# Graph attention on one core: own-block weighing and norms on ScalarE, the addition of own blocks on VectorE

## The chip, the cores and the metric

The kernel runs on one core of a Trainium2 chip. Its engines work beside each other, each with its own queue that is worked through in order: TensorE (PE, with its weight loads PEld), VectorE (DVE), ScalarE (ACT), GpSimd (POOL), and SyncE (SP), which here only issues transfers. The metric is the device time of one launch in microseconds. The kernel before took 2456.25 us, the median of three runs.

## The reference

One layer of attention over a graph, added to its input and normalised. `x` is 16 x 1024 x 512 in float32, `adj` is a 1024 x 1024 matrix of zeros and ones, the same for all 16 batches; there are 8 heads of 64.

```python
q = (x @ Wq + bq).reshape(b, n, H, HD)
k = (x @ Wk + bk).reshape(b, n, H, HD)
v = (x @ Wv + bv).reshape(b, n, H, HD)
scores = jnp.einsum('bqhd,bkhd->bhqk', q, k) / jnp.sqrt(jnp.float32(HD))
scores = scores + (1.0 - adj)[None, None, :, :] * -1000000000.0
attn = jax.nn.softmax(scores, axis=-1)
out = jnp.einsum('bhqk,bkhd->bqhd', attn, v).reshape(b, n, d)
x = _layernorm(x + out @ Wo + bo, axis=-1)
```

The matrix is sparse: most rows have few ones, the first rows have the most.

## The kernel before

The kernel does not compute the full score matrix. It lists the edges (query, key) of `adj` once, at the start (`edges`), and then handles 128 edges at a time, in a *block*. The 1024 queries of a batch are eight tiles `t` of 128. A tile has two kinds of blocks. In an *own* block each of the tile's 128 queries stands on its own partition with one of its keys; there are `OWN = (7, 3, 3, 1, 1, 2, 2, 2)` of them per tile. The edges that are left over are packed densely into *sum* blocks, `BLOCKS = (5, 2, 1, 2, 2, 1, 1, 1)` per tile, in which a partition is some edge. That is 36 blocks a batch (21 own, 15 sum) and 576 in all, tiles of 12, 5, 4, 3, 3, 3, 3 and 3 blocks.

A batch's *front* makes q, k and v of each tile: PE transposes x (L388), multiplies by the three weights (L406, four matmuls for each product), DVE adds the biases to q and k (L428, L435), ACT copies v (L441), and SP writes the rows to `q_rows` and `kv_rows` in DRAM. `norm` (L413) computes the sums of squares of each row of q and k by head: ACT squares 512 columns (L417), and one step later DVE sums them by head (L418). Their maximum is used only at the end, in a guard that chooses a general path if the scores could be too large; the values are never large here.

A block then goes through these steps. `gather` (L539, L544) issues from POOL the indirect transfers of k and v rows (`kvg`), and of q rows (`qg`) for a sum block; an own block uses the tile's q rows as they are (`qt`). `scores` multiplies q by k (L559) and sums by head (L561) on DVE. `exponentials` (L571) makes exp on ACT into the last 8 columns of the block's tile `pv`; the first block of a query tile takes `pv` from a ring of two buffers (`pv0`), all others from a ring of `PV_BUFS`. `weigh` multiplies v by these eight weights: one DVE instruction (L582), or eight on ACT, one for each head (L578). Before the change ACT does this in the first batch for odd blocks and in the last batch for two of three. An own block is added to the tile's first own block by `add_own`, on POOL (L594); a sum block goes to `add_up`, two pairs of matmuls into PSUM (L603, L604), with a 0/1 matrix that sends each edge to its query.

`normalise` adds the two parts and divides (L610 to L617, DVE), PE transposes the result (L622), ACT copies it (L626), and `finish` multiplies by Wo (L406, `po`), adds `y`, which is x + bo (POOL, L492; DVE, L499), and normalises the rows (DVE L502 to L505, POOL L508 to L510, ACT L513).

The order of the work on every engine is written by hand, by a loop over steps `n`. Step `n` emits: gathers up to block `n + 8`; `weigh(n + 1)`; `scores(n + 2)`; `normalise` of the previous tile, if block `n` is the first of a tile; whatever earlier steps have planned for this one (`later(k, fn)`); `exponentials(n + 2)`; and `add_up(n)` or `add_own(n)`. Then PE gets as much work of fronts and finishes as a credit in microseconds allows, `share` per step, with constants for the cost of each unit (`PRODUCT`, `SUM`, `TRANSPOSE`). The fronts run more than a batch ahead of the blocks and end with the mean row of v (L463 on ACT), once per batch; 34 lead-in steps come before block 0.

Of the kernel before, what the change touches and what calls it, by code (L numbers as in the profile page):

```python
# [23 lines left out]
OWN = (7, 3, 3, 1, 1, 2, 2, 2)  # L24
# [1 line left out]
DEGREE = (80, 16, 16, 16, 16, 16, 16, 16)  # L26

AHEAD = 8
KG_BUFS, QG_BUFS, QT_BUFS, PV_BUFS = 8, 5, 3, 4
NO_ROW = 65536.0  # L30

ROWS = 3
# [9 lines left out]
P = 128  # L42
# [99 lines left out]
def kernel(  # L142
# [33 lines left out]
    nc = tc.nc  # L176
    B, N, D = x.shape
    HD = D // HEADS
# [26 lines left out]
    with ExitStack() as main:  # L205
# [75 lines left out]
        def later(k, fn):  # L281
            plan.setdefault(now[0] + k, []).append(fn)
# [130 lines left out]
        def norm(b, t, i, s):  # L413
            if t == 0 and i == 0:
                NRM[b] = work.tile([P, 2, NT, HEADS], F32, tag="nrm", name=f"nrm_{b}", bufs=2)
            sq = work.tile([P, D], F32, tag="sq", name=f"sq_{b}_{t}_{i}", bufs=2)
            nc.scalar.activation(sq, s, AF.Square)  # L417
            later(1, lambda: nc.vector.tensor_reduce(  # L418
                NRM[b][:, i, t, :], sq.rearrange("p (h d) -> p h d", d=HD), axis=AX.X, op=OP.add
            ))  # L420

        def front(b, t):

# [33 lines left out]
            def mean_pe():  # L457
                p = fill_psum(f"pm_{b}")
                nc.tensor.matmul(p[0:1, :], mean, VSUM.pop(b), start=True, stop=True)

                def out():
                    m = work.tile([1, D], F32, tag="sq", name=f"mean_{b}", bufs=2)
                    nc.scalar.copy(m, p[0:1, :])  # L463
# [88 lines left out]
        def scores(n):  # L552
            b, t, i = blocks[n]
            if i < OWN[t]:
                q = QT[b, t] if i < OWN[t] - 1 else QT.pop((b, t))
            else:
                q = QG.pop(n)
            m = work.tile([P, D], F32, tag="qk", name=f"qk_{n}", bufs=2)
            nc.vector.tensor_tensor(m, q, KG[n][:, 0:D], op=OP.mult)  # L559
            S[n] = small.tile([P, HEADS], F32, tag="s", name=f"s_{n}", bufs=3)  # L560
            nc.vector.tensor_reduce(S[n], m.rearrange("p (h d) -> p h d", d=HD), axis=AX.X, op=OP.add)  # L561

        def exponentials(n):

            b, t, i = blocks[n]
            if i == 0:
                PV[n] = work.tile([P, D + HEADS], F32, tag="pv0", name=f"pv_{n}", bufs=2)
            else:
                PV[n] = work.tile([P, D + HEADS], F32, tag="pv", name=f"pv_{n}", bufs=PV_BUFS)
            bias = absent[:, own[t] + i:own[t] + i + 1] if i < OWN[t] else 0.0  # L570
            nc.scalar.activation(PV[n][:, D:], S.pop(n), AF.Exp, bias=bias)  # L571

        def weigh(n):
            v, pv = KG.pop(n), PV[n]
            b, t, i = blocks[n]
            if (b == 0 and n % 2) or (b == B - 1 and n % 3):
                for h in range(HEADS):
                    nc.scalar.activation(  # L578
                        pv[:, ts(h, HD)], v[:, ds(D + h * HD, HD)], AF.Copy, scale=pv[:, D + h:D + h + 1]
                    )  # L580
                return
            nc.vector.tensor_tensor(  # L582
                pv[:, 0:D].rearrange("p (h d) -> p h d", d=HD),
                v[:, D:].rearrange("p (h d) -> p h d", d=HD),
                pv[:, D:, None].to_broadcast([P, HEADS, HD]), op=OP.mult,
            )

        def add_own(n):
            b, t, i = blocks[n]
            pv = PV.pop(n)  # L590
            if i == 0:
                PV[b, t] = pv
            else:
                nc.gpsimd.tensor_tensor(PV[b, t], PV[b, t], pv, op=OP.add)  # L594

        def add_up(n):
            b, t, i = blocks[n]
# [47 lines left out]
        with tc.manual_schedule():  # L645
# [12 lines left out]
            while n < total or plan or urgent or done or finishing:  # L658
# [8 lines left out]
                while gathered[0] < min(n + AHEAD + 1, total) and blocks[gathered[0]][0] in set_up:  # L667
                    gather(gathered[0])
                    gathered[0] += 1
                if 0 <= n + 1 < total:  # L670
                    weigh(n + 1)
                if 0 <= n + 2 < total:
                    scores(n + 2)
                if 1 <= n <= total and (n == total or blocks[n][2] == 0):
                    normalise(*blocks[n - 1][:2])
                for fn in plan.pop(n, ()):
                    fn()
                if 0 <= n + 2 < total:
                    exponentials(n + 2)
                credit += share  # L680
                if 0 <= n < total and blocks[n][2] >= OWN[blocks[n][1]]:
                    add_up(n)
                    credit -= SUM
                elif 0 <= n < total:
                    add_own(n)
                for tile_done in done[:1]:
                    if tile_done not in Y:
                        load_y(*tile_done)
# [75 lines left out]
```

## Time and profile before

| | us |
|---|---|
| runs | 2456.4, 2456.25, 2439.39 (median 2456.25) |
| profiled execution, its own time | 2437.71 |
| span of its instructions | 2435.9 |
| POOL busy | 1560.1 |
| ACT busy | 712.8 |
| mean granted clock of TensorE | 0.957 of full speed |

A profile row of a group gives line, engine, operation, what is written and read, the count, and then busy time in us, the mean of one in ns, the idle time before them and what ended it. A timeline row gives start and duration in us. A row of stretches gives the window, its length, busy time and count of PE, PEld, DVE, ACT and POOL in that order, then granted clock, share of the DMA engines and GB/s. A row of waits gives total, count and longest in us.

### The profile page before, as it was taken

Reading aid. Unit: us, or ns where it says so; the run is one execution under the profiler, and the core shown is the slowest. Engines: PE = TensorE matmul, PEld = TensorE weight load, DVE = VectorE, ACT = ScalarE, POOL = GpSimd, SP = SyncE. Lnnn points to the kernel's source line nnn. Section 1 sums busy time; section 2 is a strip of 40 time slices with the busy share of each in tenths; the row PEclk is TensorE's granted clock in tenths of the full one; section 3 lists DMA queues with packets and bytes.
Section 4 is the critical chain, followed back from the end, with each engine's and each line's share of the span. In section 5 each row is a group of like instructions: output and inputs, shape, how many; then the busy total and the mean of one; then the engine's idle time right before and its main releaser. Section 6 shows DMA issues by size and latency. Waiting matters only on the chain.

```text
span 2435.9 us, 23939 instructions
## 1 busy us (share of the span) xinstructions
PE 2204.7 (91%) x6185; PEld 1098.5 (45%) x6185; DVE 2198.2 (90%) x3606; ACT 712.8 (29%) x1746; POOL 1560.1 (64%) x1565
## 2 busy tenths in 40 slices
PE   6988999899999989999998999999999999988555
PEld 3434445454444545444454544445454444444232
DVE  6588999899999999999999999999999999999875
ACT  2345522222222222222222222222222222222253
POOL 1055676767667676666767666576766757676683
PEclk9989999999999999999999999999999999999768
DMA  4367678687777768777776877777786767767572
GB/s 164 112 212 237 227 266 265 219 292 240 258 238 263 251 212 297 231 259 230 269 253 216 288 235 261 233 263 250 231 294 220 275 224 271 250 214 268 174 257 69
DMA packets 216639, 577.65 MB, mean 237 GB/s; under 512 B 33695, under 2 KB 33707, under 8 KB 216494
## 3 DMA queue, kind: packets, MB, share of 16 engines
q0 software_dynamic: 102144, 331.89, 42.7%
q1 hardware_dynamic: 111776, 239.16, 27.4%
q10 hardware_dynamic: 2574, 4.99, 0.6%
q8 instruction: 51, 0.84, 0.1%
q14 instruction: 94, 0.77, 0.1%
HBM read 474.75 MB, written 134.26 MB: 250 GB/s over the span
## 4 chain that ended last, share of the span: by engine, by line
DVE 42%; PE 28%; issue 16%; POOL 7%; DMA 4%; ACT 2%; POOLq 0%; ACTq 0%; SPq 0%; DVEq 0%
DVE pv L582 9%; DVE qk L559 9%; PE pv L406 7%; PE pq L406 6%; PE pk L406 6%; DVE s L561 5%; PE po L406 3%; DVE stats L502 3%; POOL kvg L544 3%; DVE y L499 3%; DVE nrm L418 3%; POOL y L492 2%; DVE o L611 2%; PE sum L603 2%; PE sum L604 2%
## 5 line engine op out<-in xcount | busy, mean ns | idle before, releaser
L544 POOL DMA_INDIRECT kvg<-kv_rows,key_row x576 | 643.3, 1117 | 348.2 <-DVE pv L582 207.7
L582 DVE TENSOR_TENSOR pv<-kvg,pv 128x512 f32<-128x512 f32 x534 | 480.7, 900 | 40.1 <-ACT pv L571 36.8
L406 PE MATMUL po<-wo,oT 128*128 128x512 f32 x1024 | 504.1, 625 | 0.0
L406 PE MATMUL pq<-wq,xT 128*128 128x512 f32 x1024 | 481.4, 602 | 23.9 <-ACT xT L392 13.1
L406 PE MATMUL pv<-wv,xT 128*128 128x512 f32 x1024 | 487.2, 611 | 0.0
L406 PE MATMUL pk<-wk,xT 128*128 128x512 f32 x1024 | 472.3, 593 | 0.0
L561 DVE TENSOR_REDUCE s<-qk 128x8 f32<-128x512 f32 x576 | 395.2, 686 | 19.9
L539 POOL DMA_INDIRECT qg<-q_rows,query_row x240 | 277.9, 1158 | 49.3 <-issue 43.7
L406 PEld LDWEIGHTS pv<-wv,xT 128*128 128x128 f32 x1024 | 201.2, 198 | 220.5 <-issue 212.7
L406 PEld LDWEIGHTS po<-wo,oT 128*128 128x128 f32 x1024 | 199.2, 202 | 202.9 <-issue 196.7
L571 ACT ACTIVATE pv<-s,absent 128x8 f32<-128x8 f32 x336 | 101.1, 301 | 629.7 <-DVE s L561 514.5
L406 PEld LDWEIGHTS pk<-wk,xT 128*128 128x128 f32 x1024 | 191.2, 190 | 206.0 <-issue 201.4
L406 PEld LDWEIGHTS pq<-wq,xT 128*128 128x128 f32 x1024 | 188.3, 193 | 198.5 <-issue 170.3
L559 DVE TENSOR_TENSOR qk<-qt,kvg 128x512 f32<-128x512 f32 x336 | 271.8, 809 | 0.0
L594 POOL TENSOR_TENSOR pv<-pv,pv 128x520 f32<-128x520 f32 x208 | 269.6, 1296 | 3.2
L508 POOL TENSOR_TENSOR rstd<-rstd,neg_half 128x1 f32<-128x1 f32 x128 | 108.5, 848 | 208.0 <-DVE rstd L505 199.1
L492 POOL TENSOR_TENSOR y<-y,bo_bc 128x512 f32<-128x512 f32 x128 | 169.4, 1323 | 110.1 <-DMA y<-in_x_dram 108.0
L603 PE MATMUL sum<-pv,sums 128*128 128x256 f32 x480 | 154.4, 405 | 91.1 <-DVE pv L582 58.5
L571 ACT ACTIVATE pv<-s 128x8 f32<-128x8 f32 x240 | 50.0, 209 | 569.1 <-DVE s L561 465.7
L603 PEld LDWEIGHTS sum<-pv,sums 128*128 128x128 f32 x480 | 92.2, 199 | 210.2 <-issue 99.3
L418 DVE TENSOR_REDUCE nrm<-sq 128x8 f32<-128x512 f32 x256 | 172.8, 676 | 1.2 <-ACT sq L417 1.2
L617 DVE TENSOR_TENSOR o<-o,rden 128x512 f32<-128x512 f32 x128 | 167.3, 1307 | 4.4
(109 smaller groups left out, 2184.2 us busy)
## 6 DMA issues: line engine op xcount, KB each, us to landing
kv_rows<-kv SPq DMA_DIRECT2D x128, 512.0 KB
x<-in_x_dram SPq DMA_DIRECT2D x128, 256.0 KB
q_rows<-q SPq DMA_DIRECT2D x128, 256.0 KB
qt<-q_rows SPq DMA_DIRECT2D x128, 256.0 KB
y<-in_x_dram SPq DMA_DIRECT2D x128, 256.0 KB
out_dram<-y SPq DMA_DIRECT2D x128, 256.0 KB
kvg<-kv_rows,key_row POOLq DMA_INDIRECT x576
a<-in_adj_dram SPq DMA_DIRECT2D x8, 512.0 KB
```

The costliest lines, as they stand in the source:

```text
L406: nc.tensor.matmul(p, lhs()[:, ts(c, P)], w[:, c, :], start=(c == 0), stop=(c == NPAIR - 1))
L418: later(1, lambda: nc.vector.tensor_reduce(NRM[b][:, i, t, :], sq.rearrange("p (h d) -> p h d", d=HD), axis=AX.X, op=OP.add))
L492: later(2, lambda: nc.gpsimd.tensor_tensor(Y[b, t], Y[b, t], bo_bc, op=OP.add))
L539: nc.gpsimd.indirect_dma_start(out=QG[n], out_offset=None, in_=q_rows[b % ROWS], in_offset=bass.IndirectOffsetOnAxis(ap=query_row[:, g:g + ...
L544: nc.gpsimd.indirect_dma_start(out=KG[n], out_offset=None, in_=kv_rows[b % ROWS], in_offset=bass.IndirectOffsetOnAxis(ap=key_row[:, g:g + ...
L559: nc.vector.tensor_tensor(m, q, KG[n][:, 0:D], op=OP.mult)
L561: nc.vector.tensor_reduce(S[n], m.rearrange("p (h d) -> p h d", d=HD), axis=AX.X, op=OP.add)
L571: nc.scalar.activation(PV[n][:, D:], S.pop(n), AF.Exp, bias=bias)
L582: nc.vector.tensor_tensor(pv[:, 0:D].rearrange("p (h d) -> p h d", d=HD), v[:, D:].rearrange("p (h d) -> p h d", d=HD), pv[:, D:, None].to ...
L594: nc.gpsimd.tensor_tensor(PV[b, t], PV[b, t], pv, op=OP.add)
L603: nc.tensor.matmul(PSUM[b, t][:, 0, 0:HD2], m, pv[:, 0:HD2], **kw)
L617: nc.vector.tensor_tensor(o8, o8, r[:, :, None].to_broadcast([P, HEADS, HD]), op=OP.mult)
```

## The change

Five things change.

- `norm` squares each head's 64 columns by itself on ACT, with the sum of squares as the instruction's second output; DVE's reduction goes.
- `by_act` says which blocks ACT weighs: own blocks except each tile's first, in all batches, and in the last batch every fourth block as well. All others are weighed on DVE.
- `add_own` adds on DVE, not on POOL.
- The order within a step: `exponentials(n + 3)` comes first, DVE's weighing of `n + 1` is followed by `scores(n + 4)`, then the addition of own block `n`, and ACT's weighing of `n + 1` comes after the planned work.
- Rings: 9 buffers for gathered k and v, not 8; 6 for `pv`, not 4; 4 for scores, not 3. `pv0` keeps its two.

```diff
-KG_BUFS, QG_BUFS, QT_BUFS, PV_BUFS = 8, 5, 3, 4
+KG_BUFS, QG_BUFS, QT_BUFS, PV_BUFS = 9, 5, 3, 6
...
         def norm(b, t, i, s):
...
-            sq = work.tile([P, D], F32, tag="sq", name=f"sq_{b}_{t}_{i}", bufs=2)
-            nc.scalar.activation(sq, s, AF.Square)
-            later(1, lambda: nc.vector.tensor_reduce(
-                NRM[b][:, i, t, :], sq.rearrange("p (h d) -> p h d", d=HD), axis=AX.X, op=OP.add
-            ))
+            for h in range(HEADS):
+                sq = work.tile([P, HD], F32, tag="sq", name=f"sq_{b}_{t}_{i}_{h}", bufs=2)
+                nc.scalar.activation(sq, s[:, ts(h, HD)], AF.Square, accum_out=NRM[b][:, i, t, h:h + 1])
...
+        def by_act(n):
+            b, t, i = blocks[n]
+            return 0 < i < OWN[t] or (b == B - 1 and n % 4 == 0)
+
         def weigh(n):
             v, pv = KG.pop(n), PV[n]
-            b, t, i = blocks[n]
-            if (b == 0 and n % 2) or (b == B - 1 and n % 3):
+            if by_act(n):
                 for h in range(HEADS):
                     nc.scalar.activation(
                         pv[:, ts(h, HD)], v[:, ds(D + h * HD, HD)], AF.Copy, scale=pv[:, D + h:D + h + 1]
...
-                nc.gpsimd.tensor_tensor(PV[b, t], PV[b, t], pv, op=OP.add)
+                nc.vector.tensor_tensor(PV[b, t], PV[b, t], pv, op=OP.add)
...
-                if 0 <= n + 1 < total:
+                if 0 <= n + 3 < total:
+                    exponentials(n + 3)
+                if 0 <= n + 1 < total and not by_act(n + 1):
                     weigh(n + 1)
-                if 0 <= n + 2 < total:
-                    scores(n + 2)
+                if 0 <= n + 4 < total:
+                    scores(n + 4)
+                if 0 <= n < total and blocks[n][2] < OWN[blocks[n][1]]:
+                    add_own(n)
                 if 1 <= n <= total and (n == total or blocks[n][2] == 0):
                     normalise(*blocks[n - 1][:2])
                 for fn in plan.pop(n, ()):
                     fn()
-                if 0 <= n + 2 < total:
-                    exponentials(n + 2)
+                if 0 <= n + 1 < total and by_act(n + 1):
+                    weigh(n + 1)
...
-                elif 0 <= n < total:
-                    add_own(n)
```

Line numbers shift a little: in the changed kernel the product of q and k is L557, its reduction L559, the exponential L569, the weighing L579 (ACT) and L583 (DVE), the own addition L595, and the head's square L418.

Where instructions stand now is seen best in the seven own blocks of a batch's first tile; in the names `pv_146` the number is that of the block (144 is the first of batch 4), and the number behind it counts instructions. DVE before, in the steps of blocks 145 and 146:

```order
L582 TENSOR_TENSOR pv_146_5416<-kvg_146_5206,pv_146_5416 128x512
L559 TENSOR_TENSOR qk_147_5437<-qt_4_0_5143,kvg_147_5242 128x512
L561 TENSOR_REDUCE s_147_5439<-qk_147_5437 128x8
L452 TENSOR_TENSOR vsum_5_5283<-vsum_5_5283,kv_5_2_5344 128x512
L428 SCALAR_TENSOR_TENSOR q_5_3_5446<-pq_5_3_5425,bq_bc_102 128x512
L582 TENSOR_TENSOR pv_147_5449<-kvg_147_5242,pv_147_5449 128x512
L559 TENSOR_TENSOR qk_148_5469<-qt_4_0_5143,kvg_148_5271 128x512
L561 TENSOR_REDUCE s_148_5471<-qk_148_5469 128x8
```

DVE in the same two steps after the change:

```order
L557 TENSOR_TENSOR qk_149_6813<-qt_4_0_6445,kvg_149_6638 128x512
L559 TENSOR_REDUCE s_149_6815<-qk_149_6813 128x8
L595 TENSOR_TENSOR pv_144_6642<-pv_144_6642,pv_145_6679 128x520
L450 TENSOR_TENSOR vsum_5_6620<-vsum_5_6620,kv_5_2_6703 128x512
L426 SCALAR_TENSOR_TENSOR q_5_3_6823<-pq_5_3_6800,bq_bc_102 128x512
L557 TENSOR_TENSOR qk_150_6852<-qt_4_0_6445,kvg_150_6675 128x512
L559 TENSOR_REDUCE s_150_6854<-qk_150_6852 128x8
L595 TENSOR_TENSOR pv_144_6642<-pv_144_6642,pv_146_6721 128x520
```

The weighing (L582) is gone from these steps, the addition (L595) has come in behind the scores, and the scores are those of two blocks later.

ACT before, from the exponential of block 147 on:

```order
L571 ACTIVATE pv_147_5449<-s_147_5439,absent_111 128x8
L513 ACTIVATE y_3_5_5326<-y_3_5_5326,rstd_5383 128x512
L417 ACTIVATE sq_5_3_0_5476<-q_5_3_5446 128x512
L626 COPY oT_3_7_5478<-poT_3_7_5454 128x512
L571 ACTIVATE pv_148_5487<-s_148_5471,absent_111 128x8
L571 ACTIVATE pv_149_5512<-s_149_5504,absent_111 128x8
```

ACT after, in the same place (the squares of q's tile 3 of the next batch):

```order
L418 ACTIVATE sq_5_3_0_0_6860,nrm_5_6275<-q_5_3_6823 128x64
L418 ACTIVATE sq_5_3_0_1_6862,nrm_5_6275<-q_5_3_6823 128x64
L418 ACTIVATE sq_5_3_0_2_6864,nrm_5_6275<-q_5_3_6823 128x64
L418 ACTIVATE sq_5_3_0_3_6866,nrm_5_6275<-q_5_3_6823 128x64
L418 ACTIVATE sq_5_3_0_4_6868,nrm_5_6275<-q_5_3_6823 128x64
L418 ACTIVATE sq_5_3_0_5_6870,nrm_5_6275<-q_5_3_6823 128x64
L418 ACTIVATE sq_5_3_0_6_6872,nrm_5_6275<-q_5_3_6823 128x64
L418 ACTIVATE sq_5_3_0_7_6874,nrm_5_6275<-q_5_3_6823 128x64
L627 COPY oT_3_7_6876<-poT_3_7_6836 128x512
L579 ACTIVATE pv_147_6768<-kvg_147_6578,pv_147_6768 128x64 x8
L569 ACTIVATE pv_150_6904<-s_150_6854,absent_111 128x8
L579 ACTIVATE pv_148_6811<-kvg_148_6606,pv_148_6811 128x64 x8
```

One square has become eight, and eight weighing instructions stand at the end of a step, in front of the next step's exponential.

The second place is the start of a three-block tile. Block 168 is the first of tile 4, block 171 the first of tile 5, and `o_4_3` is the normalised tile 3, whose `pv_165` lies in the ring of two that `pv_171` takes. ACT before:

```order
L513 ACTIVATE y_4_1_5990<-y_4_1_5990,rstd_6046 128x512
L417 ACTIVATE sq_6_0_1_6138<-kv_6_0_6109 128x512
L441 COPY kv_6_0_6109<-pv_6_0_6089 128x512
L392 COPY xT_6_2_6142<-pxT_6_2_6117 128x512
L571 ACTIVATE pv_171_6146<-s_171_6134,absent_111 128x8
```

ACT after:

```order
L627 COPY oT_4_2_7665<-poT_4_2_7639 128x512
L569 ACTIVATE pv_171_7679<-s_171_7655,absent_111 128x8
L569 ACTIVATE pv_172_7712<-s_172_7684,absent_111 128x8
L511 ACTIVATE y_4_1_7559<-y_4_1_7559,rstd_7630 128x512
L418 ACTIVATE sq_6_0_1_0_7721,nrm_6_7608<-kv_6_0_7692 128x64
```

DVE after, in the step of block 168, whose normalisation reads `pv_165`:

```order
L583 TENSOR_TENSOR pv_169_7600<-kvg_169_7404,pv_169_7600 128x512
L557 TENSOR_TENSOR qk_172_7682<-qt_4_5_7476,kvg_172_7523 128x512
L559 TENSOR_REDUCE s_172_7684<-qk_172_7682 128x8
L611 TENSOR_TENSOR rden_4_3_7687<-sum_4_3_7632,pv_165_7441 128x8
L612 TENSOR_TENSOR o_4_3_7686<-sum_4_3_7632,pv_165_7441 128x512
```

The exponential of block 171 has moved from the end of step 169 to the head of step 168, and its buffer is that of `pv_165`, so on ACT it waits for L612 of the same step. PE's and SP's instructions stand in the same order before and after.

More of the change, by code (lines that the diff above doesn't have):

```diff
@@ L461, in out @@
                 def out():
-                    m = work.tile([1, D], F32, tag="sq", name=f"mean_{b}", bufs=2)
+                    m = work.tile([1, D], F32, tag="mean", name=f"mean_{b}", bufs=1)
                     nc.scalar.copy(m, p[0:1, :])
@@ L559, in scores @@
             nc.vector.tensor_tensor(m, q, KG[n][:, 0:D], op=OP.mult)
-            S[n] = small.tile([P, HEADS], F32, tag="s", name=f"s_{n}", bufs=3)
+            S[n] = small.tile([P, HEADS], F32, tag="s", name=f"s_{n}", bufs=4)
             nc.vector.tensor_reduce(S[n], m.rearrange("p (h d) -> p h d", d=HD), axis=AX.X, op=OP.add)
```

## The prediction

> **What bounds the kernel now.** I read the page's head first, then the moments at which a batch's fronts end, the busy times of the stretches that these cut, and only then who waits for whom.
>
> ```profile
> span 2435.9 us, 23939 instructions
> PE 2204.7 (91%) x6185; PEld 1098.5 (45%) x6185; DVE 2198.2 (90%) x3606; ACT 712.8 (29%) x1746; POOL 1560.1 (64%) x1565
> L463 ACT COPY mean<-pm x16: 557/574/575, 130.4 to 2240.2; 1x512 f32<-1x512 f32 x16
> 260.28 0.57 ACT L463 COPY mean<-pm 1x512 f32<-1x512 f32 x1 [1.30 <-DVE nrm L418]
> 260.30:2240.20 1979.90, 1877.32 (x5332) 938.19 (x5330) 1863.98 (x2974) 534.73 (x1236) 1344.43 (x1346) 0.98 0.75 251
> 2240.20:2435.90 195.70, 106.43 (x246) 54.47 (x246) 139.82 (x241) 77.50 (x270) 120.70 (x132) 0.75 0.53 170
> PE sum L603 <- DVE pv L582: 54.9, 14, 5.3
> PE poT L622 <- DVE o L617: 43.2, 23, 3.6
> ```
>
> L463 runs once per batch, so it is a clock of the loop. Three of its moments (130.4, 260.3, and 2240.2 for the last of sixteen) cut the span in three: a lead-in with the first batch, 14 batches of (2240.2-260.3)/14 = 141.4 us, and a tail of 195.7 us. In the 14 batches PE is busy 1877.3 of 1979.9 us and DVE 1864.0: two engines at about 94%. PE's 102.6 us of idleness are nearly all two waits for DVE, 54.9 + 43.2 (the last two rows, of the list of waits in this stretch).
>
> How far can PE go? Its own timeline gives the price of each kind of work at full clock.
>
> ```profile
> 1011.96 0.59 PE L603 MATMUL sum<-pv,sums 128*128 128x256 f32 x2
> 1012.39 0.61 PE L604 MATMUL sum<-pv,sums 128*128 128x264 f32 x2
> 1012.84 1.88 PE L406 MATMUL pv<-wv,xT 128*128 128x512 f32 x4
> 1014.55 0.60 PE L388 MATMUL pxT<-ident,x 128*128 128x128 f32 x4
> 1014.99 3.60 PE L406 MATMUL pq<-wq,xT 128*128 128x512 f32 x8
> 1046.68 1.22 PE L603 MATMUL sum<-pv,sums 128*128 128x256 f32 x2 [5.34 <-DVE pv L582]
> L406 PE MATMUL po<-wo,oT 128*128 128x512 f32 x1024 | 504.1, 625 | 0.0
> ```
>
> From start to start: 1.71 us for four product instructions (0.43 each), 0.44 for a tile's four transposes, 0.43 + 0.45 for a sum block. A batch has 4 x 1024/16 = 256 product instructions (110.1 us), 16 groups of transposes (7.0), 15 sum blocks (13.2) and the mean (0.9): 131.2 us. So the 141.4 are 131.2 of work, 102.6/14 = 7.3 of waiting for DVE, and 2.9 of slow clock (granted 0.98). The clock falls behind long waits: after 5.34 us of idleness the same pair of matmuls took 1.22 instead of 0.59.
>
> **The change part by part.** DVE first.
>
> ```profile
> L582 DVE TENSOR_TENSOR pv<-kvg,pv 128x512 f32<-128x512 f32 x534 | 480.7, 900 | 40.1 <-ACT pv L571 36.8 <-ACT pv L578 2.1 <-issue 0.9
> L559 DVE TENSOR_TENSOR qk<-qg,kvg 128x512 f32<-128x512 f32 x240 | 166.1, 692 | 0.0
> L418 DVE TENSOR_REDUCE nrm<-sq 128x8 f32<-128x512 f32 x256 | 172.8, 676 | 1.2 <-ACT sq L417 1.2
> L594 POOL TENSOR_TENSOR pv<-pv,pv 128x520 f32<-128x520 f32 x208 | 269.6, 1296 | 3.2
> L492 POOL TENSOR_TENSOR y<-y,bo_bc 128x512 f32<-128x512 f32 x128 | 169.4, 1323 | 110.1 <-DMA y<-in_x_dram 108.0
> 1009.29 0.67 DVE L582 TENSOR_TENSOR pv<-kvg,pv 128x512 f32<-128x512 f32 x1
> 1025.34 3.47 DVE L582 TENSOR_TENSOR pv<-kvg,pv 128x512 f32<-128x512 f32 x1
> 1025.73 1.28 POOL L492 TENSOR_TENSOR y<-y,bo_bc 128x512 f32<-128x512 f32 x1
> 1026.96 1.29 POOL L594 TENSOR_TENSOR pv<-pv,pv 128x520 f32<-128x520 f32 x1
> 168.76 2.21 DVE L452 TENSOR_TENSOR vsum<-vsum,kv 128x512 f32<-128x512 f32 x1
> 2404.76 1.19 DVE L617 TENSOR_TENSOR o<-o,rden 128x512 f32<-128x512 f32 x1
> ```
>
> The weighing takes 0.67 us when nothing disturbs it and 0.90 in the mean. The row at 1025.34 shows why: it lasts 3.47 us and ends at 1028.81, 0.56 after the second of two POOL additions (1025.73 to 1028.25). A two-input DVE instruction stands still while POOL adds. I went through all DVE instructions of that kind over 0.74 us: 159 of them, from 168.76 to 2404.76 (last two rows), end 0.57 +- 0.06 us after an L594, with 204 us over 0.68 each; 47 more belong to L492, with 47 us. POOL's gathers stretch none.
>
> - L594 leaves POOL: 208 x 1.30 = 270 us of POOL, which was not the bound, and 204 us of DVE's stalls with it. Ends: 0 if another POOL instruction took its place each time, 251 if all stalls went; 204 is what the ends of the rows give.
> - The 208 additions come to DVE: by L559's row for two SBUF inputs without much stall, 208 x 0.69 = +144 (upper end 0.90 each, +187).
> - Weighing: 13 own blocks of a batch and 7 others in the last batch go to ACT, so 361 of 534 stay: -173 x 0.68 = -118.
> - L418 goes: -173.
>
> DVE in sum: -204 + 144 - 118 - 173 = -351, or 22 per batch: from 1864.0/14 = 133 to 111 us. It falls under PE's 131.
>
> ACT pays for it.
>
> ```profile
> L417 ACT ACTIVATE sq<-q 128x512 f32<-128x512 f32 x128 | 80.6, 629 | 218.6 <-DVE q L428 217.1 <-issue 1.4
> L578 ACT ACTIVATE pv<-kvg,pv 128x64 f32<-128x64 f32 x336 | 84.7, 334 | 1.3
> 162.10 1.06 ACT L298 ACTIVATE a<-a 128x1024 f32<-128x1024 f32 x1 [3.18 <-POOL codes L291]
> 163.06 0.19 ACT L298 ACTIVATION_READ_ACCUMULATOR a<-a 128x1 f32 x1
> 163.28 1.15 ACT L299 ACTIVATE a<-a,neg_one 128x1024 f32<-128x1024 f32 x1
> 165.52 0.19 ACT L300 ACTIVATION_READ_ACCUMULATOR a<-a,neg_one 128x1 f32 x1
> 165.61 2.00 ACT L578 ACTIVATE pv<-kvg,pv 128x64 f32<-128x64 f32 x8
> ```
>
> - Own weighing: 2.00 us for eight heads, 13 x 2.0 = +26 per batch.
> - Norms: 256 of 0.63 us become 2048 of 64 columns, each with a read of the accumulator behind it, as L298 has. One head costs 0.25 us (2.00/8) if the read is hidden, and 0.47 if the next one waits for the read to end, as L299 does (0.25 + 163.28 - 163.06). I take 0.34: L578 starts 0.09 behind the start of L300's read, and the new instructions wait for the one two before, not the last. Per batch 128 x 0.34 - 16 x 0.63 = +33 (ends +22 and +50).
>
> ACT per batch: 534.7/14 = 38, + 26 + 33 = 97 us (86 to 114). That is the third busy engine, and still under PE.
>
> By the Trainium skill (VectorE: DVE Perf Modes, The TRN2 errata) each ScalarE instruction pays a fixed cost, and tiles of at least 512 elements are advised; this speaks against cutting the norms. By its figure for SBUF operands (224 + 64 cycles at 1.2 GHz) a head is 240 ns by estimate, the read not counted, and ACT comes to some 85 us; the trace agrees in kind (0.334 us for 64 columns, 0.629 for 512).
>
> - New waits. The add of an own block on DVE now stands behind ACT's eight heads, which ACT issues last in the step before. Behind that add on DVE queue the normalisation (PE's poT waits for it) and the evacuations; the next block's weighing stands ahead of it, so PE's sum does not wait. The exponential of a tile's first block now reuses a buffer that the normalisation in the same step still reads, where the tile between is three blocks long (five times in a batch): ACT waits there up to a step (141.4/36 = 3.9 us), and xT, oT and v copies queue behind it. Ends 0 and 5 x 3.9 = 20 us of ACT per batch; even 97 + 20 is under 131, so I price it within PE's left-over waits below.
> - Gathers are read four steps behind their issue's step instead of six, 4 x 3.7 = 15 us; a gather read as soon as possible came 5.60 us later (row below): hidden. The middle row's DMA share, 0.75, becomes 0.75 x 141.4/134 = 0.79. The ninth key buffer and more PV buffers cost nothing but space. PE's and SP's orders do not change at all.
>
> **Sum.** With DVE at 111 and ACT at 97, PE sets the pace. Long waits become rarer, so I take a clock of 0.99, half way from 0.98 to full: 131.2/0.99 = 132.5. Of the 7.3 us of waits 1.5 stay, a fifth, my choice between 0 and 7.3: 134 per batch. 14 x (141.4 - 134) = 104 us.
>
> By the Trainium skill (TensorE: Matmul & The Clock Gate, What's actually happening) the clock halves only behind an idle window of about 3.4 us, with which 1.22 behind 5.34 idle agrees. By that rule waits under that length cost no clock, the batch is 132.7 by estimate, and the span 18 us shorter than mine.
>
> The tail is a ring of DVE and PE:
>
> ```profile
> 2261.40 1.12 PE L622 MATMUL poT<-ident,o 128*128 128x128 f32 x4 [6.39 <-DVE o L617]
> 2272.10 2.37 DVE L617 TENSOR_TENSOR o<-o,rden 128x512 f32<-128x512 f32 x1
> 2274.52 1.11 PE L622 MATMUL poT<-ident,o 128*128 128x128 f32 x4 [6.21 <-DVE o L617]
> 2345.81 5.60 DMA qg<-q_rows,query_row
> ```
>
> A tile takes 13.1 us there; L617 loses up to 2.37 - 0.67 = 1.7 us of stall, which is 14 us over some eight such tiles, and I add 6 for the additions that leave POOL in the stretch between: 20 in all (10 to 30). The first batch, PE-light, gives 5 (0 to 8). 2435.9 - 104 - 20 - 5 = 2307, and 2437.7 - 2435.9 = 1.8 around it: 2309 us. The profiled run lies 0.8% under the median of the three (2456.25) and by the fastest (2439.39); scaled to the median the sum is 2326. I give 2316.
>
> **Rivals.**
> - ACT comes late, PE waits for it. For it: the ends 0.47 per head and 20 us of waits, together 134 per batch, and lumps (six own blocks in a row). Against: the mean, 97. Then most of the 7.3 us of waits stay under another name: 136 to 139.8 a batch, 14 x 5.4 and 14 x 1.6 us saved besides the 25 of tail and first batch: 2337 to 2391 at the profiled run's level, up to 2409 at the median's; I carry it as 2345 to 2405.
> - PE is the bound already and gets nothing: its clock falls as before, and waits come from the order of its queue. Against: both waits in the list name DVE. Time within 1%, 2435 to 2455.
> - Slower: ACT becomes the bound outright. Place: the norms. Without them ACT is 54 per batch, so a batch of 145 needs (145 - 54)/128 = 0.7 us per head; there the kernel ends 14 x 3.6 = 50 us later, less the 25 of tail and first batch: from 2436 + 50 - 25 = 2461 us on. Against: 0.47 is the most that the rows bear.
> - Better than forecast: PE dense at 131.2, 30 in the tail and 8 in the first batch, 2436 - 143 - 38 + 2 = 2257.
>
> **How the numbers follow.** PE at pace, with 132.5 to 136 a batch, 2270 to 2345: 0.62. ACT late, 2345 to 2405: 0.20. No change: 0.08. Slower: 0.05. Better: 0.05. The range 2265 to 2405 holds the first two and leaves out the other three, 0.18. One per cent is about what a measurement of this kernel can tell from no change; faster by more than that has the first, second and last cases, 0.87; same 0.08; slower 0.05.
>
> **What would show it.** Right: L463's interval near 134, PE at 97% in the middle, granted clock 0.99 or more there, no DVE instruction stretched to 2 us but by L492, DVE near 111 and ACT near 97 us per batch, ACT's squares 0.34 us apart. Wrong: PE's poT or po waiting for ACT, DVE's L595 waiting long for ACT L579, ACT over 115 per batch, or squares 0.5 us and more apart.

## The result, and the profile after

The changed kernel takes 2280.73 us (median of four runs, 2278.31 to 2283.94); the kernel before, run beside it, 2452.74 (four runs). The ratio is 0.931, with a 95% interval of 0.927 to 0.935: 6.9% faster. The forecast was 2316, in a range of 2265 to 2405. The profiled execution of the changed kernel has a span of 2282.2 us, that of before 2435.9.

The page's head of the kernel after:

```profile
span 2282.2 us, 28287 instructions
PE 2157.2 (95%) x6185; PEld 1085.9 (48%) x6185; DVE 1880.6 (82%) x3385; ACT 1357.4 (59%) x6970; POOL 1280.7 (56%) x1358
```

Two of its groups of instructions (DVE's addition of own blocks, and the weighing that DVE kept), from the list that keeps shapes apart; the prediction's steps are held against them below:

```profile
L583 DVE TENSOR_TENSOR pv<-kvg,pv 128x512 f32<-128x512 f32 x361 | 252.6, 700 | 0.0
...
L595 DVE TENSOR_TENSOR pv<-pv,pv 128x520 f32<-128x520 f32 x208 | 165.0, 793 | 30.4 <-ACT pv L579 30.4
```

The once-per-batch copy, now L461, starts at 134.4, 262.5 and, for the last of sixteen, 2097.1 us, and again cuts the span. The stretches of the kernel after (window, length, busy time of PE, PEld, DVE, ACT, POOL, granted clock, DMA share, GB/s):

```profile
0.00:134.40 134.40, 113.37 (x312) 53.54 (x313) 75.52 (x137) 61.22 (x330) 19.84 (x26) 1.00 0.36 127
134.40:262.50 128.10, 109.20 (x296) 52.87 (x296) 99.75 (x240) 80.70 (x411) 63.51 (x53) 0.92 0.73 245
262.50:2097.10 1834.60, 1830.30 (x5327) 924.52 (x5326) 1568.33 (x2754) 1142.68 (x5975) 1094.13 (x1162) 1.00 0.80 270
2097.10:2282.20 185.10, 104.39 (x254) 54.95 (x254) 137.01 (x254) 72.82 (x259) 103.19 (x118) 0.77 0.54 183
```

The third row is the 14 batches: 1834.6/14 = 131.04 us each, and PE is busy 1830.3 of 1834.6 us at a granted clock of 1.00. TensorE's own work is all that is left there. The waits of that stretch (who waits for whom: total us, times, longest) agree:

```profile
PE poT L623 <- DVE o L618: 4.2, 2, 4.0
...
DVE y L497 <- POOL y L490: 91.6, 48, 4.4
...
DVE pv L595 <- ACT pv L579: 29.1, 35, 2.1
...
ACT pv L569 <- DVE o L612: 285.9, 82, 9.6
```

PE's 102.6 us of idleness have become 4.3, and of these one wait has 4.0. It stands behind a wait of DVE for `y`, as DVE's and PE's timelines say:

```profile
433.65 0.69 DVE L497 TENSOR_TENSOR y<-po,y 128x512 f32<-128x512 f32 x1 [4.41 <-POOL y L490]
438.45 0.63 PE L623 MATMUL poT<-ident,o 128*128 128x128 f32 x4 [3.96 <-DVE o L618]
```

The other engines do wait, ACT for 286 us in front of exponentials whose buffer the normalisation still reads, but beside that one wait for `y` almost nothing of it reaches PE.

By stretch the span lost 1979.9 - 1834.6 = 145.3 us in the 14 batches and 195.7 - 185.1 = 10.6 in the tail, and gained 262.5 - 260.3 = 2.2 before them: 153.7.

Where in a batch was it won? PE's order is the same in both kernels, so the moment at which a tile's `poT` starts can be compared tile by tile. Worked out from those rows of L622 (before) and L623 (after), as means over twelve batches: from the last tile's `poT` to tile 0's it was 48.53 us and is 42.62; tiles 1 to 4 take 18.08, 16.55, 10.91 and 10.04 in both kernels, to the hundredth; tiles 5 to 7 took 12.05, 13.31 and 12.20 and take 10.98, 10.97 and 11.00. So before the change PE ran at its own pace through tiles 1 to 4, and lost 5.9 us in tile 0, with its seven own blocks in a row, and 4.6 in tiles 5 to 7, where two blocks of three are own.

### The profile page after: what moved, and what is told of

It reads as the page before. It is cut to its first block, busy times and chain, and to the rows that moved or that the text cites. A ratio compares the mean times of both kernels' runs of the same rounds, so it can differ in the third digit from the quotient of the medians.

```text
span 2282.2 us, 28287 instructions
## 1 busy us (share of the span) xinstructions
PE 2157.2 (95%) x6185; PEld 1085.9 (48%) x6185; DVE 1880.6 (82%) x3385; ACT 1357.4 (59%) x6970; POOL 1280.7 (56%) x1358
## 5 line engine op out<-in xcount | busy, mean ns | idle before, releaser
L406 PE MATMUL pv<-wv,xT 128*128 128x512 f32 x1024 | 474.2, 597 | 4.9 <-ACT sq L418 4.9
L579 ACT ACTIVATE pv<-kvg,pv 128x64 f32<-128x64 f32 x1720 | 432.5, 337 | 0.2 <-issue 0.2
L559 DVE TENSOR_REDUCE s<-qk 128x8 f32<-128x512 f32 x576 | 395.2, 686 | 22.3
L418 ACT ACTIVATE sq<-q 128x64 f32<-128x64 f32 x1024 | 246.5, 243 | 164.1 <-DVE q L426 148.4
L569 ACT ACTIVATE pv<-s,absent 128x8 f32<-128x8 f32 x336 | 97.7, 295 | 406.6 <-DVE o L612 341.1
L418 ACT ACTIVATE sq<-kv 128x64 f32<-128x64 f32 x1024 | 246.1, 242 | 84.8 <-DVE kv L433 63.9
L537 POOL DMA_INDIRECT qg<-q_rows,query_row x240 | 257.4, 1072 | 58.5 <-issue 56.4
L583 DVE TENSOR_TENSOR pv<-kvg,pv 128x512 f32<-128x512 f32 x361 | 252.6, 700 | 0.0
L557 DVE TENSOR_TENSOR qk<-qt,kvg 128x512 f32<-128x512 f32 x336 | 239.6, 713 | 8.6 <-DMA kvg<-kv_rows,key_row 8.6
L497 DVE TENSOR_TENSOR y<-po,y 128x512 f32<-128x512 f32 x128 | 88.0, 687 | 131.8 <-POOL y L490 101.2
L418 ACT ACTIVATION_READ_ACCUMULATOR sq<-q 128x1 f32 x1024 | 192.1, 188 | 0.0
L418 ACT ACTIVATION_READ_ACCUMULATOR sq<-kv 128x1 f32 x1024 | 191.9, 187 | 0.0
```

What stands on the lines that cost most here:

```text
L406: nc.tensor.matmul(p, lhs()[:, ts(c, P)], w[:, c, :], start=(c == 0), stop=(c == NPAIR - 1))
L418: nc.scalar.activation(sq, s[:, ts(h, HD)], AF.Square, accum_out=NRM[b][:, i, t, h:h + 1])
L497: nc.vector.tensor_tensor(y, p, y, op=OP.add)
L537: nc.gpsimd.indirect_dma_start(out=QG[n], out_offset=None, in_=q_rows[b % ROWS], in_offset=bass.IndirectOffsetOnAxis(ap=query_row[:, g:g + ...
L579: nc.scalar.activation(pv[:, ts(h, HD)], v[:, ds(D + h * HD, HD)], AF.Copy, scale=pv[:, D + h:D + h + 1])
L583: nc.vector.tensor_tensor(pv[:, 0:D].rearrange("p (h d) -> p h d", d=HD), v[:, D:].rearrange("p (h d) -> p h d", d=HD), pv[:, D:, None].to ...
```

## Experiments

Three theories were set against each other first. Mine, from the prediction: VectorE's total load decides. Against it: the stalls behind GpSimd's additions decide; or the look-ahead does. Four kernels make one part of the change each, on the kernel before.

**d_add**: the kernel before with the additions on DVE.

```diff
-                nc.gpsimd.tensor_tensor(PV[b, t], PV[b, t], pv, op=OP.add)
+                nc.vector.tensor_tensor(PV[b, t], PV[b, t], pv, op=OP.add)
```

> The kernel before, with the addition of own blocks moved from GpSimd to VectorE and nothing else. If VectorE's total load decides (133 us per batch before, stalls of 12.7 away, 13 additions of 0.69 = 9 new): VectorE near 130, batch interval 133 to 135 us. If the stalls behind GpSimd's additions are what decides: 131 to 133. If the look-ahead of scores and exponentials decides: 138 to 141.

**d_norm**: with the squares by head on ACT.

```diff
...
-            nc.scalar.activation(sq, s, AF.Square)
-            later(1, lambda: nc.vector.tensor_reduce(
...
+            for h in range(HEADS):
...
+                nc.scalar.activation(sq, s[:, ts(h, HD)], AF.Square, accum_out=NRM[b][:, i, t, h:h + 1])
```

In d_norm and in u_norm below, the buffer of the once-per-batch copy moves with the norms, as it does in the change itself: with the old norms the copy takes one from the ring of `sq`, with the new ones it has its own.

> The kernel before, with the norms squared and summed by head on ScalarE and nothing else. If VectorE's total load decides (133 - 16 x 0.68 = 122 per batch): interval 132 to 134 us. If the stalls behind GpSimd's additions decide: 137 to 141, since these stay. If the look-ahead decides: 138 to 141.

**d_weigh**: with the own blocks weighed on ACT, in the old order.

```diff
-            if (b == 0 and n % 2) or (b == B - 1 and n % 3):
+            if 0 < i < OWN[t] or (b == B - 1 and n % 4 == 0):
```

> The kernel before, with own blocks (but each tile's first) weighed on ScalarE and nothing else; the order of a step is that of before. If VectorE's total load decides (133 - 13 x 0.7 to 0.9 = 121 to 124 per batch): interval 132 to 134 us. If the stalls decide: 137 to 141. If the look-ahead decides: 138 to 141, or longer than 141.4, since ScalarE's eight heads now stand ahead of the step's other work.

**d_order**: with the new order of a step and the larger rings, and nothing else.

```diff
-KG_BUFS, QG_BUFS, QT_BUFS, PV_BUFS = 8, 5, 3, 4
+KG_BUFS, QG_BUFS, QT_BUFS, PV_BUFS = 9, 5, 3, 6
...
-                    scores(n + 2)
+                    scores(n + 4)
...
-                    exponentials(n + 2)
+                    exponentials(n + 3)
```

> The kernel before with the new order of a step alone (exponentials three ahead, scores four ahead, rings of 9, 6 and 4): additions on GpSimd, norms reduced on VectorE and ScalarE's share of the weighing as before. If VectorE's load decides, it is unchanged at 133 per batch: interval 139 to 141.4 us. If the look-ahead decides: 131 to 133.

Then four that undo one part of the changed kernel each: **u_add** puts the additions back on POOL, **u_norm** the old norms, **u_order** the old order and rings; **u_weigh** has this edit, the old rule of what ACT weighs:

```diff
-            return 0 < i < OWN[t] or (b == B - 1 and n % 4 == 0)
+            return (b == 0 and n % 2 == 1) or (b == B - 1 and n % 3 != 0)
```

> The changed kernel with the additions of own blocks on GpSimd again. VectorE loses 13 additions per batch (165/16 = 10 us) and gets the stalls behind GpSimd's additions back; with own weighing alone moved 139 stalls of 141 us in all were left. 'Stalls behind GpSimd decide': interval 134 or more, ratio over 0.945. 'VectorE within a tile decides': the stalls bring about what the additions take away, VectorE 110 to 114 per batch: interval 131 to 132, ratio 0.93 to 0.94.

> The changed kernel with the norms as before: one square of 512 columns on ScalarE and a sum by head on VectorE. 'VectorE within a tile decides': tile 0 holds about a third of a batch's 16 norms, 5 x 0.68 = 3.4 more on VectorE, 38.2 of 42.6: interval 131 to 132, ratio 0.93 to 0.94. 'Norms are needed': VectorE's 112 per batch become 123, and the interval goes to 133 or more, ratio over 0.945. The lead-in should be some 3 to 4 us shorter in either case, since it was with every kernel that kept the old norms.

> The changed kernel with the steps' old order (scores and exponentials two steps ahead, the addition last in its step, the old numbers of buffers); additions on VectorE, own weighing and norms on ScalarE stay. 'The order is needed for what ScalarE was given': with the norms alone moved, VectorE waited 103 us for the exponentials, which stood behind the eight squares of a norm in ScalarE's queue, and with 26 us per batch more of weighing in that queue it waits at least as long: waits of VectorE for exponentials over 100 us, interval 134 to 139, ratio 0.945 to 0.98, though VectorE's total is 112 us a batch. 'VectorE within a tile decides by its busy time alone': interval 131 to 132, ratio 0.93 to 0.94, since the order alone was worth nothing (0.9996).

> The changed kernel with the own blocks of tile 0 and of the other tiles weighed on VectorE again (as before: on ScalarE only in part of the first and last batch); additions on VectorE, norms on ScalarE and the new order stay. What each theory expects. 'The own weighing decides' (it alone gave 0.938): without it most of the gain goes, interval of a batch 137 to 139 us, ratio to before 0.96 to 0.98. 'VectorE within a tile decides' (the time is lost only where VectorE's instructions of one tile's steps, its stalls counted, take longer than TensorE's 42.6 us of tile 0 and 11 us of tiles 5 to 7): VectorE has 34.8 us in tile 0 of the changed kernel and gets six weighings of 0.68 back, 38.9, still under 42.6, and two more in the other tiles 5 to 7 at most one each: interval 131 to 132, ratio 0.93 to 0.94, VectorE some 121 us a batch - the same total as with the norms alone moved, which ran at 139.4.

What these eight gave, with the four kernels that followed from them. Interval is that of the once-per-batch copy over 14 batches; DVE's busy time is that of the row of these 14 batches, over 14; the waits are DVE's for POOL's y and for ACT's part of a block, the exponential or the eight heads (and 8.5 us in all for an output transfer in u_add), in the same stretch, over 14. The three kernels d_norm, d_add and d_weigh have two runs each, the others four or more.

| kernel | ratio to before (95%) | interval, us | DVE busy per batch | DVE waits for y and ACT's `pv` per batch |
|---|---|---|---|---|
| before | | 141.4 | 133.1 | 4.6 |
| d_order | 1.000 (0.997 to 1.002) | 142.1 | 131.5 | 3.7 |
| d_norm | 0.985 (0.980 to 0.990) | 139.4 | 120.9 | 15.0 |
| d_add | 0.965 (0.960 to 0.970) | 137.8 | 130.6 | 4.0 |
| d_weigh | 0.938 (0.932 to 0.944) | 132.0 | 120.8 | 7.2 |
| u_add | 0.969 (0.964 to 0.974) | 135.7 | 111.8 | 13.7 |
| u_weigh | 0.964 (0.959 to 0.968) | 136.5 | 120.2 | 10.0 |
| u_norm | 0.935 (0.931 to 0.939) | 131.6 | 122.1 | 5.3 |
| u_order | 0.929 (0.925 to 0.933) | 130.9 | 111.7 | 8.3 |
| after | 0.931 (0.927 to 0.935) | 131.0 | 112.0 | 8.6 |
| before_y | 0.980 (0.977 to 0.983) | 138.5 | 133.3 | 1.5 |
| u_weigh_y | 0.932 (0.929 to 0.935) | 130.9 | 122.6 | 0.0 |
| u_add_y | 0.932 (0.929 to 0.935) | 130.4 | 115.1 | 0.1 |
| best | 0.925 (0.922 to 0.928) | 130.6 | 115.2 | 4.5 |

All three first theories fall: each missed at least one of the four. The look-ahead alone is worth nothing, and d_add's 137.8 lies in no range that was given for it. The stalls alone aren't it: d_weigh keeps 141 us of stalls behind POOL's additions (139 DVE instructions, counted as in the prediction) and has nine tenths of the gain. And DVE's total isn't it, as d_norm and d_weigh show. The 14 batches of d_norm in the view of stretches:

```profile
265.50:2217.10 1951.60, 1866.25 (x5331) 931.93 (x5329) 1692.08 (x2748) 819.73 (x4567) 1347.73 (x1345) 0.99 0.76 254
```

and DVE's waits in them:

```profile
DVE pv L580 <- ACT pv L569: 108.5, 129, 2.4
DVE y L497 <- POOL y L490: 101.6, 55, 4.6
```

The same two views of d_weigh:

```profile
259.98:2108.30 1848.32, 1835.07 (x5329) 923.13 (x5327) 1691.77 (x2797) 873.99 (x2644) 1318.18 (x1345) 1.00 0.80 268
```

```profile
DVE y L499 <- POOL y L492: 81.4, 49, 4.0
DVE pv L582 <- ACT pv L571: 19.3, 37, 1.4
```

DVE is busy 1692 us in both, and the batches take 139.4 and 132.0 us. The difference of 7.4 us a batch is about what their waits differ by, (210.1 - 100.7)/14 = 7.8. With the norms alone on ACT, DVE's weighing waits 129 times for the exponential, which in the old order is issued behind the squares. A wait at the head of its queue takes DVE's time as an instruction does. In five kernels of the old order, busy time and these waits together fall short of the interval by nearly the same 3.2 to 4.0 us (before 137.7 of 141.4, d_add 134.6 of 137.8, d_norm 135.9 of 139.4, d_weigh 128.0 of 132.0, before_y 134.8 of 138.5). That is a count that fits, not a proof: in d_weigh PE is busy 131.1 of the 132.0 us, so it is nearly the floor there, as it is in u_order, and in the new order the count leaves more over (d_order 6.9, u_weigh 6.3, u_add 10.2). The proof for the waits for y comes with the kernels below that take them away.

The table also shows what the changed kernel needs. Without the norms or without the order it can't be told from the whole change by its ratio. So neither by itself is needed, against the expectations of 133 us or more for u_norm and 134 to 139 for u_order. In u_order DVE waited 59.9 us for exponentials, where over 100 were expected. Without the weighing or without the additions it loses over 3 points, though DVE is busy only 120 and 112 us a batch. They were to stay at 131 to 132 us if DVE's busy time within a tile decided, so that theory, my second one, falls as well. In u_weigh DVE's largest wait is for y. One such place in its timeline:

```profile
1078.96 1.19 SPq L489 DMA_DIRECT2D y<-in_x_dram  x1
...
1087.58 1.26 POOL L490 TENSOR_TENSOR y<-y,bo_bc 128x512 f32<-128x512 f32 x1 [8.77 <-DMA y<-in_x_dram]
1088.37 0.58 ACT L461 COPY mean<-pm 1x512 f32<-1x512 f32 x1 [3.21 <-PE pm L457]
1088.88 0.69 DVE L497 TENSOR_TENSOR y<-po,y 128x512 f32<-128x512 f32 x1 [4.01 <-POOL y L490]
```

The load of y is issued at 1078.96; 8.62 us later it is there. POOL has stood 8.77 us in front of it, with its gathers behind, and DVE 4.01 us, with everything behind. The kernel before has this row among DVE's waits in its 14 batches, and the prediction did not price it:

```profile
DVE y L499 <- POOL y L492: 37.8, 40, 3.8
```

So three kernels load y earlier, at the tile's normalisation instead of when its `oT` is done, about three steps, with eight buffers for y in place of six. POOL's addition follows the load by two steps and so moves with it; load, addition and buffers were not tried apart. PE's order stays as it is. **u_weigh_y** and **u_add_y** are u_weigh and u_add with this edit, **before_y** the kernel before with nothing else:

```diff
...
-            Y[b, t] = work.tile([P, D], F32, tag="y", name=f"y_{b}_{t}", bufs=6)
-            loaded[b, t] = now[0]
+            Y[b, t] = work.tile([P, D], F32, tag="y", name=f"y_{b}_{t}", bufs=8)
...
         def normalise(b, t):
+            load_y(b, t)
             s, pv = PSUM.pop((b, t)), PV.pop((b, t))
...
-                    if tile_done not in Y:
-                        load_y(*tile_done)
+                    loaded.setdefault(tile_done, n)
```

> u_weigh (own weighing on VectorE, the rest as in the changed kernel; interval 136.5 us) with each y tile loaded at the tile's normalisation, some three steps earlier, in one of eight buffers instead of six; TensorE's order is the same. 'Late y': VectorE's queue stood 140 us in the 14 batches in front of the add of the projection, for GpSimd's y, which waits for the load; that is 10 us a batch, and with the load earlier the interval falls to 131 to 132.5, ratio to before 0.93 to 0.94. 'Own blocks': a step of the run of own blocks needs 3 x 0.69 + 0.68 us of VectorE for its block and about 1 us of other work, more than the 3.64 us (131/36) that TensorE takes for a step, and where VectorE waits for y it has nothing to catch up: the waits for y go, but the interval stays at 135 to 136.5, ratio 0.955 to 0.965.

> u_add (additions of own blocks on GpSimd in the new order; interval 135.7 us) with the same earlier load of y. GpSimd waits there 164 us in front of its additions for ScalarE's weighing, with gathers and y behind it, and VectorE waits 178 us for GpSimd's y. 'Late y': interval 131 to 132.5, ratio 0.93 to 0.94, though GpSimd's additions still stop VectorE some 150 us. 'Stalls behind GpSimd's additions': interval stays at 134.5 or more, ratio over 0.955.

> The kernel before with nothing but the earlier load of y (at the tile's normalisation, eight buffers). 'Late y is what bound the kernel before too': interval 131 to 134, ratio 0.93 to 0.955, and the change would have been a detour. 'VectorE's time with its stalls': before, VectorE is busy 133 us a batch, 251 us of it in the 14 batches and around them stalls behind GpSimd's additions, and waits for GpSimd's y only 37 us, 2.7 a batch: an earlier y can save at most those 2.7 and leaves an interval of at least 137, ratio 0.975 to 1.00; the stalls stay about 250 us in all.

The 14 batches of u_weigh in the view of stretches, and the waits of PE and DVE there:

```profile
264.30:2175.20 1910.90, 1853.79 (x5330) 929.63 (x5329) 1682.85 (x2930) 820.70 (x4574) 1098.86 (x1162) 0.99 0.77 259
```

```profile
PE poT L623 <- DVE o L618: 42.0, 18, 4.1
PE sum L604 <- DVE pv L583: 12.8, 12, 1.3
...
DVE y L497 <- POOL y L490: 140.1, 45, 6.4
```

The same of u_weigh_y, with PE's only wait and POOL's for the load; DVE has no row for y any more:

```profile
265.40:2098.50 1833.10, 1830.36 (x5332) 924.45 (x5331) 1716.39 (x2931) 818.04 (x4575) 1105.15 (x1162) 1.00 0.80 270
```

```profile
PE poT L623 <- DVE o L618: 2.6, 4, 1.0
...
POOL y L489 <- DMA y<-in_x_dram: 195.4, 40, 8.3
```

POOL still stands 195 us in front of the loads, but DVE no longer waits for it at all, and PE is dense: 136.5 us a batch have become 130.9 (131 to 132.5 expected), with DVE busier than in u_weigh (122.6 against 120.2). The same holds for u_add_y. Its 14 batches, and what POOL still waits for there:

```profile
269.10:2094.90 1825.80, 1825.80 (x5318) 922.95 (x5317) 1611.74 (x2572) 1144.06 (x5975) 1344.29 (x1343) 1.00 0.80 271
```

```profile
POOL pv L594 <- ACT pv L578: 159.2, 54, 6.2
```

DVE's stalls behind POOL's additions are 238 us there (216 instructions, behind own blocks and y), nearly the 251 of before and more than the 150 that were expected, and PE loses nothing to them. So late y took what u_weigh and u_add lost: shown. The kernel before is another case. The 14 batches of before_y, and PE's waits in them:

```profile
261.80:2201.00 1939.20, 1862.12 (x5332) 932.10 (x5330) 1866.43 (x2974) 534.26 (x1236) 1339.42 (x1344) 0.99 0.77 256
```

```profile
PE sum L602 <- DVE pv L581: 42.5, 14, 3.8
PE poT L622 <- DVE o L617: 33.7, 23, 2.7
```

An early y takes 141.4 - 138.5 = 2.9 us from its batch, as much as its waits for y (37.8/14 = 2.7); DVE, busy 133.3 us a batch with its stalls, still sets the pace, as the second theory of that expectation had it (the stalls came to 263 us by the same count, expected about 250). That is more than PE's own 131. So before the change VectorE's busy time was the bound, and some of it had to go before PE could run dense.

Last, a kernel that takes what the others showed: u_order with the early y, and with the first batch's norms summed on DVE as before, since with the squares by head the first copy came some 4 us later (what that mark is worth is said below).

```diff
...
+            if b == 0:
+                sq = work.tile([P, D], F32, tag="sq0", name=f"sq_{b}_{t}_{i}", bufs=2)
+                nc.scalar.activation(sq, s, AF.Square)
+                later(1, lambda: nc.vector.tensor_reduce(
+                    NRM[b][:, i, t, :], sq.rearrange("p (h d) -> p h d", d=HD), axis=AX.X, op=OP.add
+                ))
+                return
             for h in range(HEADS):
...
```

> u_order (the steps' old order with additions on VectorE, own weighing and norms on ScalarE; interval 130.9, first mark 135.3) with y loaded earlier as in the other two, and the first batch's norms summed on VectorE as before, since every kernel with the old norms had its first mark some 4 us earlier. TensorE has no idle time left in the middle (130.9 of 130.9 at full clock), so nothing is to be won there by either theory: interval 130.8 to 131.1; lead-in 3 to 5 us shorter, tail 182 to 185: ratio 0.924 to 0.929.

It takes 2266.86 us (2263.97 to 2268.34). Its four runs all lie under the four of the changed kernel, 0.6% in the median; the two were not run side by side, and the intervals of their ratios just touch. By the profiled spans it is 20.1 us shorter: 9.1 ahead of the 14 batches (253.4 against 262.5 us), 4.7 behind them (180.4 against 185.1), and 6.3 in them, which are at PE's work in both. Its first copy comes at 132.7 us, 2.6 earlier than u_order's 135.3, where 3 to 5 were expected; the interval, 130.6, and the tail lie a little under the ranges given.

## Why the prediction was right, and where it was wrong

- **The middle.** Forecast 134 us a batch with PE setting the pace; measured 131.04. The direction and the bound were right, and three terms were too large. The clock came to 1.00, not 0.99; of the 1.5 us of left waits 0.3 remained; and PE was busy 1830.3/14 = 130.7 us, not 131.2 (0.43 is 1.71/4 rounded up, which makes 0.6 over 256 instructions). That is 41.4 us over 14 batches; with the tail's 9.4 and the first batch's 7.2 the other way, the sum of 2309 becomes 2284, the profiled execution's time. That the sum missed by 25 us and not by 41 is luck: the last two errors took away part of the first. The Trainium skill (TensorE: Matmul & The Clock Gate, What's actually happening) lets the clock halve behind an idle window of about 3.4 us; the estimate by it, 132.7 a batch, was nearer than mine. Behind the one wait of 4.0 us the trace agrees: from 438.9 to 442.4 us the granted clock was 0.51. That shorter waits cost no clock is not borne out: the longest wait of PE in d_weigh's 14 batches is 2.83 us, and from 445.96 to 449.37, around its end, the clock was 0.52.
- **"With DVE at 111 and ACT at 97, PE sets the pace."** The conclusion held and the reason was too coarse. DVE came to 112.0 a batch. But d_norm, at 120.9, and u_add, at 111.8, lie under PE's 131 as well and run at 139.4 and 135.7. DVE's waits at the head of its queue belong to its time; the prediction left out those for y, and of the new waits that it named, those of DVE for ACT's eight heads came to 29 us, the longest 2.1, and the one long wait left on PE stands behind y.
- **DVE's terms.** Forecast -351 us, measured 2198.2 - 1880.6 = -317.6. The addition costs 0.793 us (L595), not 0.69, 165 against 144 us: y's additions on POOL still stop it. Those stalls grew from 47 to 62.5 us (52 instructions). The 204 us behind own additions went to zero as forecast.
- **ACT.** A head's square with its read takes 0.24 us, below my low end of 0.25, where I had taken 0.34. ACT is at 1142.68/14 = 81.6 us a batch, not 97. Its waits for the normalisation's buffer came to 285.9/14 = 20.4 us a batch, the upper end that was given (82 of them, up to 9.6 us, where five a batch of up to 3.9 were reckoned), and 81.6 + 20.4 is still far under 131. The square's timeline in the kernel after:

```profile
1008.72 0.24 ACT L418 ACTIVATE sq<-q 128x64 f32<-128x64 f32 x1
1008.87 0.19 ACT L418 ACTIVATION_READ_ACCUMULATOR sq<-q 128x1 f32 x1
1008.96 0.24 ACT L418 ACTIVATE sq<-q 128x64 f32<-128x64 f32 x1
1009.10 0.19 ACT L418 ACTIVATION_READ_ACCUMULATOR sq<-q 128x1 f32 x1
1009.20 0.24 ACT L418 ACTIVATE sq<-q 128x64 f32<-128x64 f32 x1
```

  The read starts 0.15 us behind its square and lies beside the next one. The Trainium skill (VectorE: DVE Perf Modes, The TRN2 errata) gave 240 ns a head by estimate from its figures, and the trace agrees.
- **The tail.** Forecast -20, measured -10.6. The step that failed is the 14 us for L617, 1.7 of stall for each of some eight tiles. In the tail of before only six of its 13 were stretched, three of them to about 2.4 us and three to 1.2, and the whole group lost 5.6 us, as its rows in the tails of before and after say. That leaves 5.0 of the 10.6 for the rest, near the 6 that was added. PE's poT waited 39.4 us for this instruction in the tail of before and waits 30.1 now.

```profile
L617 DVE TENSOR_TENSOR o<-o,rden 128x512 f32<-128x512 f32 x13 | 15.7, 1209 | 0.4
...
L618 DVE TENSOR_TENSOR o<-o,rden 128x512 f32<-128x512 f32 x13 | 10.1, 775 | 0.4
```

  So the ring of DVE and PE still holds, and ACT waits 50.5 us for the normalisation's buffer; which of the two holds the tail was not tried. Waits in the tail of the kernel after:

```profile
PE poT L623 <- DVE o L618: 30.1, 8, 4.4
...
ACT pv L569 <- DVE o L612: 50.5, 8, 8.2
```

- **The first batch.** Forecast -5, measured +2.2 at the second copy. The first copy comes 4 us later (130.4 to 134.4): all kernels with the old norms have it at 130.2 to 131.1, and all with the norms on ACT throughout at 133.1 to 135.5. But that copy stands in ACT's queue, and PE had lost nothing by then: the product that it reads starts at 124.88 before and 124.72 after (first two rows). From there to the same product of the next batch (two rows of stretches, before and after) PE took 2.8 us longer, busy 2.1 more for its work at a clock of 0.92 instead of 0.93, and idle 0.6 more.

```profile
124.88 1.02 PE L459 MATMUL pm<-vsum,mean 128*1 128x512 f32 x2
124.72 1.02 PE L457 MATMUL pm<-vsum,mean 128*1 128x512 f32 x2
...
124.88:255.92 131.04, 111.73 (x312) 54.10 (x311) 113.78 (x252) 65.52 (x179) 74.65 (x61) 0.93 0.68 224
124.72:258.52 133.80, 113.85 (x311) 55.11 (x310) 103.48 (x256) 83.96 (x412) 65.62 (x53) 0.92 0.67 222
```

  One wait there is for the squares, 4.9 us at 158.9. Yet u_norm, with the old norms, has its second copy at 262.8, no earlier than the changed kernel's 262.5, so the norms don't explain the 2.2; what does stays open.

```profile
PE pv L406 <- ACT sq L418: 4.9, 1, 4.9
```

- **The rivals.** ACT late: no; PE never waited for ACT in the 14 batches. PE the bound already: no, as the tiles show. The slower case needed 0.7 us a head; it was 0.24.

What stays open: in the new order DVE's busy time and waits leave more of the interval over than in the old one (10 us in u_add, 6 to 7 in u_weigh and d_order, where the old order has 3 to 4). That y is what u_add and u_weigh lost was shown; why the same microseconds cost more was not tried.

## What to carry to other kernels

Add to an engine's busy time its waits at the head of its queue before comparing it with another engine's: two kernels with the same 1692 us of VectorE took 139.4 and 132.0 us a batch, and their waits differed by about as much. Then take a wait away and see: in u_weigh it gave 5.5 us a batch, in u_order 0.3. Where a late load (here y, 8.6 us from issue to use) is waited for in the in-order queue of the engine that sets the pace, try an earlier issue beside moving arithmetic: with it, either of two parts of this change could be left out. And cut the loop at a landmark that PE passes in the same order in both kernels: tile by tile it told where the 10 us of a batch were lost, which no total could. A mark on another engine can move by itself: ScalarE's first copy came 4 us later while PE had lost nothing.

## What the runs showed of the hardware

The read of an accumulator (0.19 us) costs ScalarE almost nothing behind a short square: eight squares with reads start 0.24 us apart. VectorE's stalls behind GpSimd's additions are no loss by themselves: in u_add_y, with 238 us of them, VectorE was busy 115.1 us a batch, stalls counted, under TensorE's 130.4, and in the kernel before, with 251, it was busy 133.1, over TensorE's work. The stalls behind y's additions alone went from 47 us before to 97 in d_add, where nothing but the own additions left GpSimd, and to 62.5 in the changed kernel, 116 in u_weigh_y and 147 in u_add_y, though the number of these additions is the same. So what VectorE gains by taking an addition off GpSimd can't be reckoned from the stalls behind that addition alone. Around the end of a wait of TensorE of only 2.83 us (d_weigh) the granted clock was 0.52 over 3.4 us.
